# Later, chained residual sums, one unit's sums on VectorE and ScalarE's norms behind its chain, in a convolution and attention kernel on Trainium2

## The chip, the core and the metric

The kernel runs on one core of a Trainium2 chip. The metric is the device time of one execution in microseconds (us), the median of three runs. The core's engines are TensorE (PE in the profile, its weight loads PEld), VectorE (DVE), ScalarE (ACT), GpSimd (POOL) and SyncE (SP), which here only issues DMAs. Each engine runs its instructions in the order of its program: an instruction that waits for a semaphore holds up everything behind it on the same engine.

## What is computed

Eight images of 512 channels by 32x32 pixels go through two layers, all in float32. Cut to what matters:

```
t  = silu(bn(conv1x1(groupnorm(x))));  ys = [t[:256], t[256:]]
for i in 0, 1:                                   # the two blocks
    z = silu(bn(conv3x3(ys[-1])))
    q, k, v = conv1x1(z)                         # 4 heads of 64 channels
    z = softmax(q (k + r) / 8) v                 # over the 1024 pixels
    ys.append(ys[-1] + silu(bn(conv1x1(z))))     # residual sum of conv_m2
x2 = x + silu(bn(conv1x1(concat(ys))))           # residual sum of conv2
out = x2 + permuted_sparse_conv1x1(groupnorm(x2))
```

## The kernel before

**Units.** The attention of one image and block is cut into four units (2 head pairs by 2 halves of the query pixels), 64 units in all. A unit has eight tiles of keys, t = 0 to 7. For each tile TensorE makes the logits of two heads (`lg`, L510), ScalarE copies them to SBUF (`st`, L517), and VectorE takes a running maximum from the PSUM bank (`mx`, L522). After the eighth tile TensorE transposes the maximum, VectorE reduces it (`nm`) and TensorE spreads it (`mb`). Then `soften` on VectorE adds the negated maximum to the tile (L544), `exponent` on ScalarE takes the exponential (L548), GpSimd adds the tile to a running sum in four pieces of 256 columns (`sum`, L555), and TensorE multiplies it with the values (`po`, L562). At the end TensorE reduces the sum over partitions (`den`), ScalarE copies it (`rb`), and VectorE takes the reciprocal and writes the product into `q` (L583 and L585).

**Order of the work.** The unit loop (L1048 to L1086) mixes the softens, exponentials and values of one unit with the logits of the next. Four units form a slot; the images go in pairs, (0,1), (2,3), (4,5), (6,7), each with the slots block 0 of both images and then block 1 of both. Between the tiles of the units a filler (L912) brings in the other work, in steps that a planner's clock paces: `advance` runs generators until a share of the planned time is used, and `clock.at` puts a function off by a planned delay. The filler's work is `conv_m2` of block outputs, the 3x3 convolution as six products (`m` with `plane`, L313), the projection to q, k and v, and a background list: `conv1` of later images, `conv2` and the last convolution of earlier ones.

**Who may pass whom.** A scheduler orders each engine's program by the program's order and its dependencies. Three helpers fix parts of it by hand: `in_turn` chains VectorE's maxima, softens and transform steps, `act_turn` chains ScalarE's copies and exponentials, `pe_turn` chains TensorE's logits, values and transposes. In the kernel before the residual sums and the group norms' `apply` are in none of these chains, so the scheduler puts them where their inputs are due by its plan.

**The lines the change touches.** `apply` (L165) normalises one 128x512 half tile in place on ScalarE, for `norm_x` (L237, the input x) and `norm_x2` (L473, the sum x2). `conv_m2` (L416) loads the residual from DRAM into a tile `res`, multiplies, applies SiLU on ScalarE into `m2s` (L130), and adds on VectorE (L430): into `ybuf` for block 0, in place into `res` for block 1; the sum is stored by SyncE. `conv2` (L443) does the same with `xr` and `cv2s` (L457), then takes group norm statistics (L139), and stores the pair after its second half. `res`, `xr` and the last convolution's `x2r` share a pool `gr` of two buffers; `m2s`, `cv2s`, `y` and `rb` share a pool of three; all 128x512 PSUM results share five banks (`ps_f`). All loads and stores go through SyncE's one queue of instructions. `GroupNorm.mean` and `var` (L141 to L162) end in small VectorE steps on 128x4 numbers (`gms`, `gd`, `gvs`, `go`) and two small matmuls (`gm`, `gv`).

## Time and profile before

| | us |
|---|---|
| three runs | 3157.03, 3156.82, 3152.05 |
| median | 3156.82 |
| the profiled execution | 3162.82 |
| its span, first to last instruction | 3161.1 |

The span holds 34185 instructions. The mean granted TensorE clock is 0.996 of full speed. Apart from PE and PEld, the busy times are: DVE 2049.9 us, ACT 1721.0, POOL 1398.4. In the profile a group line of the timeline reads: start, duration, engine, line of the kernel, operation, output <- inputs by the program's names, shapes, number of instructions; in square brackets the idle time of the engine just ahead of it and what ended that. Times are counted from the span's start. The work of a pair of images repeats with a period of 709 us: a place at 992 us comes again at 1702 and 2411.

### The profile page before, as it was taken

What the parts mean: (1) busy time and instruction counts of PE and PEld (TensorE: products, weight loads), DVE (VectorE), ACT (ScalarE), POOL (GpSimd) and SP (SyncE); (2) the same over time, 40 slices, a digit from 0 to 9 for tenths busy, and PEclk for the clock granted to TensorE, in tenths of its full rate; (3) what the DMA queues carried; (4) which work ended last, traced back from release to release, by engine and by line L of the source; (5) the groups of instructions that cost most, each with busy time, mean ns of one, the idle gap of its engine ahead of it and who ended that gap; (6) DMA issues with size and microseconds to landing.
All of it is one profiled execution on the core that took longest, in us unless ns stands there. A gap on an engine that the chain in (4) does not pass through costs nothing.

```text
span 3161.1 us, 34185 instructions
## 1 busy us (share of the span) xinstructions
PE 3077.0 (97%) x11668; PEld 1515.3 (48%) x11668; DVE 2049.9 (65%) x2718; ACT 1721.0 (54%) x2349; POOL 1398.4 (44%) x1867
## 2 busy tenths in 40 slices
PE   7999999998999999999999999999999999999999
PEld 3645354454445454455445454454445454453333
DVE  5446577567667576667666676767666676767642
ACT  3245765855655555644656455544656455546621
POOL 2104444546444554455444454445444464444520
PEclk9999999999999999999999999999999999999999
DMA  8852352421233232424233332424233332413356
GB/s 289 292 182 74 130 180 87 153 77 63 88 116 131 79 128 71 149 84 148 84 116 130 114 127 70 153 85 136 91 110 130 120 120 70 150 64 120 120 205 217
DMA packets 142014, 399.35 MB, mean 126 GB/s; under 512 B 13072, under 2 KB 14352, under 8 KB 141840
## 3 DMA queue, kind: packets, MB, share of 16 engines
q1 hardware_dynamic: 141120, 396.94, 36.6%
q8 instruction: 92, 1.51, 0.2%
q14 instruction: 82, 0.67, 0.1%
q10 hardware_dynamic: 720, 0.23, 0.0%
HBM read 317.42 MB, written 79.69 MB: 126 GB/s over the span
## 4 chain that ended last, share of the span: by engine, by line
PE 75%; DVE 4%; ACT 4%; issue 2%; DMA 1%; POOL 1%; SPq 0%; ACTq 0%; DVEq 0%; POOLq 0%
PE cv L175 15%; PE m L313 13%; PE po L562 12%; PE lg L510 12%; PE l L175 7%; PE qk L175 6%; PE v L405 3%; PE m L175 3%; PE den L576 2%; PE mb L539 2%; PE mt L530 1%; ACT st L517 1%; DVE st L544 1%; ACT st L548 1%; DVE mx L522 1%
## 5 line engine op out<-in xcount | busy, mean ns | idle before, releaser
L555 POOL TENSOR_TENSOR sum<-sum,st 128x256 f32<-128x256 f32 x1536 | 1132.0, 771 | 552.1 <-ACT st L548 547.7
L522 DVE TENSOR_TENSOR mx<-mx,lg 128x512 f32<-128x512 f32 x768 | 477.8, 682 | 417.6 <-ACT st L517 417.4
L517 ACT COPY st<-lg 128x512 f32<-128x512 f32 x1024 | 525.0, 597 | 356.1 <-PE lg L510 331.7
L548 ACT ACTIVATE st<-st 128x1024 f32<-128x1024 f32 x512 | 539.1, 1068 | 304.1 <-DVE st L544 302.9
L544 DVE TENSOR_TENSOR st<-st,mb 128x1024 f32<-128x1024 f32 x512 | 604.4, 1215 | 60.2 <-PE mb L539 60.2
L555 POOL TENSOR_TENSOR sum<-st,st 128x256 f32<-128x256 f32 x256 | 185.1, 754 | 788.8 <-ACT st L548 788.8
L313 PE MATMUL m<-plane,w_m 128*128 128x256 f32 x2304 | 528.8, 383 | 4.9 <-ACT cv2s L130 2.7
L562 PE MATMUL po<-st,v 128*64 128x512 f32 x2048 | 497.8, 605 | 18.2 <-ACT st L548 16.2
L510 PE MATMUL lg<-q,k 64*128 64x512 f32 x2048 | 510.9, 617 | 2.9 <-ACT y L130 2.9
L313 PEld LDWEIGHTS m<-plane,w_m 128*128 128x128 f32 x2304 | 426.4, 189 | 129.5 <-issue 45.1
L175 PE MATMUL cv<-y,w_cv 128*128 128x512 f32 x1024 | 464.5, 599 | 7.9 <-ACT cv2s L130 4.6
L510 PEld LDWEIGHTS lg<-q,k 64*128 64x128 f32 x2048 | 177.3, 186 | 328.2 <-issue 267.4
L175 PEld LDWEIGHTS cv<-y,w_cv 128*128 128x128 f32 x1024 | 185.8, 190 | 248.1 <-issue 226.4
L562 PEld LDWEIGHTS po<-st,v 128*64 128x64 f32 x2048 | 128.8, 136 | 323.6 <-issue 237.3
L175 PE MATMUL cv<-x,w_cv 128*128 128x512 f32 x512 | 237.0, 610 | 10.6 <-ACT y L130 3.7
L175 PE MATMUL l<-x,w_l 128*128 128x512 f32 x512 | 236.9, 606 | 7.9 <-DVE mx L522 6.9
L175 PE MATMUL qk<-z,w_qkv 128*128 128x512 f32 x512 | 234.0, 600 | 1.4 <-DVE mx L522 1.4
L583 DVE RECIPROCAL rb<-rb 128x256 f32<-128x256 f32 x128 | 215.5, 1723 | 26.0 <-ACT rb L579 25.8
L531 DVE TENSOR_REDUCE nm<-mt 128x4 f32<-128x512 f32 x128 | 82.3, 684 | 144.7 <-PE mt L530 144.7
L579 ACT COPY rb<-den 128x512 f32<-128x512 f32 x64 | 37.3, 583 | 230.4 <-PE den L576 230.4
L175 PEld LDWEIGHTS cv<-x,w_cv 128*128 128x128 f32 x512 | 95.3, 194 | 132.0 <-issue 109.3
L175 PEld LDWEIGHTS l<-x,w_l 128*128 128x128 f32 x512 | 93.4, 191 | 130.4 <-issue 112.2
(145 smaller groups left out, 2408.8 us busy)
## 6 DMA issues: line engine op xcount, KB each, us to landing
w_m<-w_m SPq DMA_DIRECT2D x96, 768.0 KB, 4.8
w_cv<-in_cv SPq DMA_DIRECT2D x90, 512.0 KB, 3.5
y<-y SPq DMA_DIRECT2D x64, 512.0 KB, 4.8
x<-in_x SPq DMA_DIRECT2D x56, 512.0 KB, 5.2
y<-y SPq DMA_DIRECT2D x64, 256.0 KB, 3.5
k<-r SPq DMA_DIRECT2D x32, 512.0 KB, 3.6
res<-y SPq DMA_DIRECT2D x32, 512.0 KB, 4.0
xr<-in_x SPq DMA_DIRECT2D x32, 512.0 KB, 4.1
```

The source lines that it names most:

```text
L175: nc.tensor.matmul(ps, w, moving, start=(n == 0), stop=(n == len(terms) - 1))
L313: nc.tensor.matmul(ps[:, ts(co, 256)].rearrange("p (t x) -> p t x", x=F), w[:, co, c, dx], u[:, 9 * c : 9 * c + 8, dx : dx + F], start=(j ...
L405: nc.tensor.matmul(ps[:, ts(j, P)], z[:, c, ts(4 * j4 + j, P)], w[:, c, 512 + P * hp : 512 + P * hp + P], start=(c == 0), stop=(c == IT - 1),)
L510: nc.tensor.matmul(lg[h], self.k[r, ts(t, P)], self.q[r, self.hp, ts(self.half, HALF)], start=True, stop=True)
L517: act_turn(nc.scalar.copy(st[:, h], lg[h]))
L522: in_turn(nc.vector.tensor_tensor(self.mx[:, h], so_far[:, h], lg[h], ALU.max))
L531: nc.vector.tensor_reduce(self.nm[:, h], mt, AX.X, ALU.max, negate=True)
L544: in_turn(nc.vector.tensor_tensor(st, st, flat(self.mb), ALU.add))
L548: act_turn(nc.scalar.activation(st, st, AF.Exp))
L555: nc.gpsimd.tensor_tensor(flat(self.acc)[:, part], flat(so_far)[:, part], st[:, part], ALU.add)
L562: nc.tensor.matmul(self.po[HD * h : HD * h + HD], self.v[:, t, ts(h, HD)], self.st[t][:, h], start=(t == 0), stop=(t == KT - 1),)
L583: nc.vector.reciprocal(self.rb[:, r], self.rb[:, r])
```

## The change

Residual sums are kept back. A new class `Later` holds a list of closures; each is due a planned delay after it is added (2.0 us of the planner's clock in `conv_m2`, 3.0 in `conv2`), runs in the order of the list, and all that remain are run ahead of the last step of the generator. Each sum is put into VectorE's chain by `in_turn`; its store, and for `conv2` the statistics, come with it. `conv2` now yields after every channel group in the same way. The last of the 64 units adds each tile to its sum with one VectorE instruction of 128x1024 in the chain, where the other units keep four GpSimd instructions of 128x256. The group norms' `apply` gets a dependency of order on the last copy or exponential that ScalarE's chain has emitted so far: it can't run ahead of that instruction. Nothing else is changed; what is computed is the same.

```diff
         def apply(self, k, dst, src):
-            nc.scalar.activation(dst, src, AF.Identity, bias=self.off[:, k : k + 1], scale=self.rstd[:, k : k + 1])
+            return nc.scalar.activation(
+                dst, src, AF.Identity, bias=self.off[:, k : k + 1], scale=self.rstd[:, k : k + 1]
+            )
...
+    def act_behind(instruction):
+
+        if act_last:
+            tc.add_manual_dep(instruction.ins, act_last[0].ins.name, IN_ORDER, reason="order of ScalarE")
+
...
+    class Later:
+
+
+        def __init__(self, delay):
+            self.delay, self.waiting = delay, []
+
+        def add(self, f):
+            self.waiting.append(f)
+            clock.at(self.delay, lambda: self.upto(f))
+
+        def upto(self, f):
+            while f in self.waiting:
+                self.waiting.pop(0)()
+
+        def flush(self):
+            if self.waiting:
+                self.upto(self.waiting[-1])
...
         def norm_x(self, tiles, k=None):
-            for k in range(CT) if k is None else (k,):
-                t = tiles[k // 2][:, k % 2]
-                self.gn0.apply(k, t, t)
+            for j in range(CT) if k is None else (k,):
+                t = tiles[j // 2][:, j % 2]
+                act_behind(self.gn0.apply(j, t, t))
...
             q = self.q
+            later = Later(2.0)
...
                     dst = y_rows(co, h) if i == 0 else res[:, co]
-                    nc.vector.tensor_tensor(dst, res[:, co], t, ALU.add)
-                    load(y_dram[n][2 + i][:, co, ts(h, HALF)], dst)
+
+                    def add(h=h, co=co, dst=dst, src=res[:, co], t=t):
+                        in_turn(nc.vector.tensor_tensor(dst, src, t, ALU.add))
+                        load(y_dram[n][2 + i][:, co, ts(h, HALF)], dst)
+
+                    later.add(add)
+                    if (h, co) == (1, IT - 1):
+                        later.flush()
                     yield us
...
+            later = Later(3.0)
...
                     bn_silu(t, ps, BN_CV2 + co)
-                    nc.vector.tensor_tensor(res[:, c], res[:, c], t, ALU.add)
-                    self.gn1.stats(co, h, res[:, c])
-                    if c == 0:
-                        yield us
-                load(x2_dram[n][:, h, 2 * cp : 2 * cp + 2], res)
-                yield us
+
+                    def add(cp=cp, c=c, co=co, res=res, t=t):
+                        in_turn(nc.vector.tensor_tensor(res[:, c], res[:, c], t, ALU.add))
+                        self.gn1.stats(co, h, res[:, c])
+                        if c == 1:
+                            load(x2_dram[n][:, h, 2 * cp : 2 * cp + 2], res)
+
+                    later.add(add)
+                    if (cp, c) == (1, 1):
+                        later.flush()
+                    yield us
...
             t = tiles[k // 2][:, k % 2]
-            self.gn1.apply(k, t, t)
+            act_behind(self.gn1.apply(k, t, t))
...
                 self.acc = pair(one, "acc", f"sum_{self.name}")
+            if t and self is units[-1]:
+
+                so_far = self.st[0] if t == 1 else self.acc
+                in_turn(nc.vector.tensor_tensor(flat(self.acc), flat(so_far), st, ALU.add))
+                return
             for j in range(4 if t else 0):
```

## The prediction

> **What bounds the kernel now.** I read the busy shares first, then the waits of TensorE in the timeline, stretch by stretch, then what each of them waited for.

> ```profile
> PE 3077.0 (97%) x11668; PEld 1515.3 (48%) x11668; DVE 2049.9 (65%) x2718; ACT 1721.0 (54%) x2349; POOL 1398.4 (44%) x1867
> L544 DVE TENSOR_TENSOR st<-st,mb 128x1024 f32<-128x1024 f32 x512 | 604.4, 1215 | 60.2 <-PE mb L539 60.2
> ```

> TensorE is busy for 3077.0 of 3161.1 us. So all of its idle time is 84 us, and an edit pays or costs only where it moves a TensorE wait. The program's work on TensorE stays the same. The other engines have time to spare on average, but each runs in order: what counts is which instruction stands ahead of the one that TensorE waits for. I therefore compared the built programs' orders on each engine and walked each place where it changed through the timeline. Only the following places move a TensorE wait.

> **Early norms and banks (gain).** In two places a SiLU that frees a PSUM bank stands behind a table load and an exponential (380.33 us: the bank of `y`; 609.73 us: of `m2s`):

> ```profile
> 378.20 1.28 ACT L130 ACT_TABLE_LOAD   x1
> 379.50 0.78 ACT L130 ACTIVATE y<-cv,bn_b,bn_s 128x512 f32<-128x512 f32 x1
> 380.33 1.12 PE L175 MATMUL cv<-x,w_cv 128*128 128x512 f32 x2 [2.16 <-ACT y L130]
> 609.73 2.62 PE L175 MATMUL cv<-x,w_cv 128*128 128x512 f32 x4 [2.13 <-ACT m2s L130]
> ```

> With the norms behind the chain, the built program runs both SiLUs ahead of that exponential, next to another SiLU, and saves two loads of 1.28. The SiLU then ends by 377.5 and 606.1, before TensorE wants the bank, so 2.1 goes at each; what is late next (the exponentials, wanted 3 to 7 us after they end) has slack. Behind 609.73 TensorE also ran at half clock for a 3.4 us stretch (granted 0.64 over 609.7 to 614.5), worth 1.7. Two smaller waits of `y` and `po` (187.41 and 527.14, 1.5 each) lose their cause but meet DMA waits soon after: I take 0.5 of at most 3. Together -6.4 (ends 0 and -9).

> **cv2s ahead of an exponential (gain).** At 1259.53 a bank waits 0.77 for `cv2s`, which now precedes the exponential; three pairs of images: 3 x -0.7 = -2.1 (0 to -2.3).

> **The last unit (gain).**

> ```profile
> 3009.41 16.46 POOL L555 TENSOR_TENSOR sum<-sum,st 128x256 f32<-128x256 f32 x24 [1.20 <-ACT st L548]
> 3016.98 8.90 DVE L150 TENSOR_TENSOR gd_b<-mv_b,gms_b 128x4 f32<-128x4 f32 x1
> 3026.33 0.59 PE L156 MATMUL gv_b<-gd_b,gmat 128*128 128x4 f32 x2 [5.90 <-DVE gd_b L152]
> 3026.78 5.76 PE L175 MATMUL l<-x,w_l 128*128 128x512 f32 x8
> ```

> A subtraction of four columns takes 8.90 us and ends as GpSimd's 24 sums end; TensorE waits 5.90 for it, then does 8 passes in 5.76 where 3.70 is usual. The change takes 28 sums off GpSimd and puts 7 x 1.22 = 8.5 us on VectorE (the duration of a soften, the same shape). Walking VectorE's new order, softens and sums alternate and `gd` is done at 3023.1, so the matmul comes 3.2 earlier; the 8 passes may run at full clock (2.0). The wait that is left, 2.7, is of a size that was followed by half clock at 609.73 and not at 380.33, so I take 1.3 of the 2.0: -4.5 (ends -3.0 and -6.9). What is late next is `den`, for which the last sum ends at 3025.7, before it is wanted.

> [...]

> **Second residual of block 1, images 1, 3, 5 (loss).** This decides. The view is the timeline around 990 us, by engine:

> ```profile
> 984.88 1.23 DVE L430 TENSOR_TENSOR res<-res,m2s 128x512 f32<-128x512 f32 x1
> 991.40 1.22 DVE L544 TENSOR_TENSOR st<-st,mb 128x1024 f32<-128x1024 f32 x1
> 992.53 2.10 DVE L430 TENSOR_TENSOR res<-res,m2s 128x512 f32<-128x512 f32 x2
> 988.49 0.52 SPq L78 DMA_DIRECT2D res<-y  x1
> 987.44 1.06 ACT L548 ACTIVATE st<-st 128x1024 f32<-128x1024 f32 x1
> 988.40 2.03 ACT L517 COPY st<-lg 128x512 f32<-128x512 f32 x4
> 990.30 1.09 ACT L548 ACTIVATE st<-st 128x1024 f32<-128x1024 f32 x1
> 987.14 5.45 PE L313 MATMUL m<-plane,w_m 128*128 128x256 f32 x24
> 992.52 1.94 PE L562 MATMUL po<-st,v 128*64 128x512 f32 x8
> ```

> The second half's `res` takes the first half's buffer, so its load is issued at 988.49, when the first half's store has landed (issued 986.14, 2.33), and lands at 992.40. In the program before, softens 2 and 3 ran from 982.62, ahead of it. In the changed program both stand behind all four sums, and `in_turn` forbids them to pass. The wait that is added is VectorE's, for the load; queued behind it are softens 2 and 3, then maxima and softens 4 and 5. Without the soften ahead, the store is issued some 0.4 earlier: load landed at 992.0, two sums to 993.7, softens to 994.9 and 996.1. Exponential 2 ends at 996.0 instead of 988.50: `po` wants it at 992.52 and waits 3.5. Then ScalarE makes its four copies (2.0), then exponential 3 (1.1): 999.1, where before `po` 3 went at 993.43. TensorE is late by 5.6; the trace has 0.2 of slack at most, I take 5.4. The same rows stand at 1702 and 2411 us: 3 x 5.4 = +16.2. Ends: +3 each if only the first wait stays, +8 if half clock follows it, as behind this wait of 3.0 at 219:

> ```profile
> 219.00:222.40 3.40, 3.39 (x8) 1.18 (x8) 0.00 (x0) 1.25 (x2) 0.00 (x0) 0.50 0.71 248
> ```

> (Columns: window, length, busy time of PE, PEld, DVE, ACT and POOL, clock, DMA.) The cover was 5.45 us of 3x3 products, and it is used up.

> **Block 0, images 3, 5, 7 (loss).**

> ```profile
> 1301.67 1.88 DVE L522 TENSOR_TENSOR mx<-mx,lg 128x512 f32<-128x512 f32 x3 [2.29 <-ACT st L517]
> 1307.08 0.69 DVE L430 TENSOR_TENSOR ybuf<-res,m2s 128x512 f32<-128x512 f32 x1 [3.52 <-DMA res<-y]
> 1316.01 1.98 PE L175 MATMUL l<-x,w_l 128*128 128x512 f32 x4 [2.48 <-DVE mx L522]
> ```

> The third sum waits for its load (1299.82 to 1307.05). Three maxima run ahead of it now; in the changed order all four stand behind it, and the first frees the bank that TensorE takes at 1302.41. The load is issued at 1299.4, one store and not two ahead of it; from the 3.9 us of the load at 988 and the 7.2 of this one I bound its landing by 1303.3 and 1306.6. At 1304 the bank comes at 1305.2: +2.8. The wait at 1316.01 takes about half of that back; then soften 6 stands behind a sum of `xr` that waits for `cv2s`, and the bank wanted at 1323.96 comes some 3 late. So 3 x 3 = +9 (ends 0, if the later waits take it all back, and +5 each).

> **Block 0, images 2, 4, 6 (loss).** The load of `res` lands at 1131.18; softens 4 and 5, which ran at 1121.26 to 1123.61, now stand behind it. The load goes out 1.4 sooner (1124.5); landed at 1129 to 1129.8, exponentials 4 and 5 are in time for `po` at 1135.12, but soften 6, `cv2s` and the plane of `m` follow late: 1141 to 1143 where TensorE began at 1139.89. 3 x 2 = +6 (0 to +3 each).

> **The rest.** Everywhere else the sums of `conv_m2` and `conv2` move by a few places with their inputs long there; the `po` that follows has 3 us of 3x3 products ahead of it, as at 1514.73 to 1520.11. I cost these at nothing; without that cover each would cost one sum, 0.7 to 1.2. The stores and loads move in SyncE's queue with their sums; the store of a `conv2` pair goes out about 1 later, and the pair stored at 1321.41 is not loaded again before 1383.

> **Sum:** -6.4 - 2.1 - 4.5 + 16.2 + 9 + 6 = +18.2 us. The profiled execution took 3162.82, so it would take 3181.0; it lies 6.0 above the median of the runs, 3156.82, from which the sum gives **3175.0**. About 6 us (0.2%) is what a measurement of this kernel can tell from no change.

> **Rivals.**

> (1) *Faster: the cover at 990 us holds.* If the second `res` lands before the softens matter, all four sums pass without a wait, and the same goes for block 0. Place: the load issued at 988.49. Price: the three losses vanish, and -13.0 is left: 3144. It decides at a landing of 988.7: two sums (1.4), soften 2 (1.2) and its exponential (1.1) then end at 992.5, when `po` is wanted. For it: nothing in the change delays that load. Against it: the load would need to land 3.3 sooner than I derive, and it needs the store ahead of it. 0.14.

> (2) *No change.* Only the first wait at 990 stays (+3 x 3) and block 0 costs 1 each (+6): +2.0, 3158.8. It needs the copies of ScalarE to go ahead of exponential 2, against the order of its chain. 0.14.

> (3) *My forecast*, 3164 to 3188. For it: every step is an order that the built program fixes and a transfer whose time is in the trace. 0.52.

> (4) *The clock gate follows.* The waits of 3.5 at 990 and of 2.7 at the end bring half clock (1.7 per stretch of 3.4 us) and the block 0 places cost their upper ends: +8 x 3, +5 x 3, +3 x 3, with the gains of 11.6 (the last unit at -3.0): +36, 3193. 0.15. [...]

> (5) *The last unit gains nothing*, since VectorE's own seven sums hold the subtraction as GpSimd's did: +4.5, 3179.5; inside my range for (3). 0.05.

> **How the numbers follow.** The predicted time is that of (3), 3175. Faster by over 0.2% is (1): 0.14, and I add 0.02 from the edge of (2). Within 0.2% is the rest of (2): 0.12. Slower is (3), (4) and (5): 0.72. The range leaves out (1) and the upper quarter of (4): from 3151, below (2), to 3196.

> **What would show it.** In the profile after: `po` waits of about 3.5 and 2 us for the exponential near 990, 1702 and 2411 (shifted by what came before), VectorE idle there for a DMA of `res` ahead of its sums; the gain at 380 and 610 as missing waits; `gd` no longer 8.90, and `gv`'s wait below 3 us. I am wrong if `po` runs through at 990, if half clock follows these waits (then it is more), or if the early gains come back as DMA waits.

## The result, and the profile after

The changed kernel takes 3203.09 us (median of 4 runs, 3201.45 to 3205.92) where the kernel before took 3155.54 beside it (4 runs): a ratio of 1.0150, 95% interval 1.0137 to 1.0163, so 47.5 us slower. The forecast was 3175, range 3151 to 3196. The profiled execution took 3204.52, 41.7 more than the profiled execution of before; where the other 6 us are is said with the fifth experiment (e5).

The busy times and two costly groups on the page of the changed kernel (L586 is the exponential, L605 the product with the values; the columns at the end are busy time, mean, idle time just before them and what ended it):

```profile
PE 3100.5 (97%) x11668; PEld 1521.7 (48%) x11668; DVE 2041.3 (64%) x2725; ACT 1716.2 (54%) x2345; POOL 1371.9 (43%) x1839
L586 ACT ACTIVATE st<-st 128x1024 f32<-128x1024 f32 x512 | 539.6, 1069 | 353.8 <-DVE st L582 348.9
L605 PE MATMUL po<-st,v 128*64 128x512 f32 x2048 | 509.7, 609 | 33.3 <-ACT st L586 25.4
```

TensorE does the same 11668 matmuls, but its busy time is 23.5 higher, part of which is half clock, as shown below. `po`'s idle time for exponentials went from 16.2 to 25.4, and the exponentials' for softens from 302.9 to 348.9. Of the kernel before (who waited for whom, us in total, times, longest):

```profile
ACT st L548 <- DVE st L544: 302.9, 130, 7.1
PE po L562 <- ACT st L548: 16.2, 14, 3.7
```

To find the rest I compared the start of each TensorE instruction in the two traces and noted each place where the lag, the difference of the two starts, jumps.

**Block 1, images 1, 3, 5: +8.4, +8.2, +8.4, together 25.** The timeline of the changed kernel at the first of them, by engine: VectorE (L458 the residual sum, L582 soften), ScalarE, TensorE.

```profile
982.70 1.28 DVE L458 TENSOR_TENSOR res<-res,m2s 128x512 f32<-128x512 f32 x1 [2.12 <-ACT m2s L130]
990.58 1.29 DVE L458 TENSOR_TENSOR res<-res,m2s 128x512 f32<-128x512 f32 x2 [6.59 <-DMA res<-y]
991.79 2.34 DVE L582 TENSOR_TENSOR st<-st,mb 128x1024 f32<-128x1024 f32 x2
...
993.03 1.06 ACT L586 ACTIVATE st<-st 128x1024 f32<-128x1024 f32 x1 [7.72 <-DVE st L582]
994.00 2.03 ACT L555 COPY st<-lg 128x512 f32<-128x512 f32 x4
995.89 1.09 ACT L586 ACTIVATE st<-st 128x1024 f32<-128x1024 f32 x1
...
994.14 1.97 PE L605 MATMUL po<-st,v 128*64 128x512 f32 x4 [3.67 <-ACT st L586]
997.03 1.97 PE L605 MATMUL po<-st,v 128*64 128x512 f32 x4 [0.92 <-ACT st L586]
```

This is the chain of the prediction, step for step: VectorE stands 6.59 for the load of the second half, the softens come behind it, then an exponential, then ScalarE's four copies, and only then the next exponential; `po` waits twice. The two waits and the overlap between them cost 5.3 to 5.9 at each of the three places (the lag at the second group of `po`). The other 2.5 to 2.9 come behind it, while TensorE runs at half clock. The stretches of the changed kernel around it (length, busy time of PE, PEld, DVE, ACT, POOL, then clock, DMA share, GB/s):

```profile
990.30:994.00 3.70, 0.17 (x1) 0.00 (x0) 3.42 (x4) 0.97 (x2) 0.00 (x0) 0.81 0.58 158
994.00:997.40 3.40, 2.34 (x6) 0.59 (x8) 3.40 (x7) 2.98 (x6) 3.06 (x5) 0.50 0.64 227
997.40:1000.80 3.40, 3.40 (x8) 0.85 (x6) 1.98 (x2) 1.06 (x1) 3.40 (x6) 0.50 0.18 69
```

TensorE is empty for 3.5 us, then works at 0.50 through the next 6.8. The mean of 0.81 over the first 3.70 says that half clock began about 1.4 before its end, at 992.6, when TensorE (last work at 985.02 + 5.45) had been empty for 2.1.

**Block 0, images 3, 5, 7: +4.5, +7.0, +3.4.** VectorE and TensorE of the changed kernel (L560 is the maximum, L177 a convolution, L338 the 3x3 product):

```profile
1313.92 0.69 DVE L458 TENSOR_TENSOR ybuf<-res,m2s 128x512 f32<-128x512 f32 x1 [2.81 <-ACT st L555]
1314.53 2.47 DVE L560 TENSOR_TENSOR mx<-mx,lg 128x512 f32<-128x512 f32 x4
...
1315.27 3.70 PE L177 MATMUL cv<-y,w_cv 128*128 128x512 f32 x8 [2.96 <-DVE mx L560]
1328.33 1.98 PE L177 MATMUL l<-x,w_l 128*128 128x512 f32 x4 [0.95 <-DVE mx L560]
1337.95 3.29 PE L338 MATMUL m<-plane,w_m 128*128 128x256 f32 x14 [1.94 <-DVE x2r L524]
```

All four maxima stand behind the third sum, as predicted. The releaser named at 1313.92 is a ScalarE copy that the sum does not read. The load of `res`, issued at 1308.88, took 5.0 to land, so until 1313.9, and e11 below, without the load, has no wait of `cv` there.

**Block 0, images 2, 4, 6: +3.2, +3.0, +1.4**, a wait of 2.9 of the 3x3 products at 1148.30 and its like. The second sum waits for its load, and from there to the plane that the products read (until 1148.19) VectorE is idle for 0.47 alone:

```profile
1135.86 1.29 DVE L458 TENSOR_TENSOR ybuf<-res,m2s 128x512 f32<-128x512 f32 x2 [4.88 <-DMA res<-y]
1146.95 1.24 DVE L307 TENSOR_TENSOR plane<-a,b 128x544 f32<-128x544 f32 x1
1148.30 2.09 PE L338 MATMUL m<-plane,w_m 128*128 128x256 f32 x7 [2.91 <-ACT st L555]
```

**Places that the prediction does not have: six waits of `qk`, +0.75 each.** VectorE of the changed kernel at the first one (L492 is `conv2`'s sum):

```profile
843.75 1.28 DVE L492 TENSOR_TENSOR xr<-xr,cv2s 128x512 f32<-128x512 f32 x1 [0.66 <-ACT cv2s L130]
844.96 1.21 DVE L582 TENSOR_TENSOR st<-st,mb 128x1024 f32<-128x1024 f32 x1
...
847.82 2.46 DVE L560 TENSOR_TENSOR mx<-mx,lg 128x512 f32<-128x512 f32 x4
```

and TensorE, which wants the bank that the first maximum frees:

```profile
848.54 3.70 PE L177 MATMUL qk<-z,w_qkv 128*128 128x512 f32 x8 [0.48 <-DVE mx L560]
```

In the program before, two softens and only then the sum stand there, and `qk` goes on without a wait:

```profile
842.02 2.35 DVE L544 TENSOR_TENSOR st<-st,mb 128x1024 f32<-128x1024 f32 x2
846.62 1.29 DVE L457 TENSOR_TENSOR xr<-xr,cv2s 128x512 f32<-128x512 f32 x1 [0.66 <-ACT cv2s L130]
848.95 3.27 PE L175 MATMUL qk<-z,w_qkv 128*128 128x512 f32 x7
```

Now the sum, which waits for `cv2s`, goes ahead of both softens, and its statistics go between them.

**Gains.** The stalls at 380.33 and 609.73 are gone (the lag falls by 2.2 and 3.9 there), but around 342 and 400 to 426 the lag rises by 2.4 and 4, at waits that lead back to DMAs of `x`. The bank of `cv2s` gives 0.8 three times.

### The profile page after: what moved, and what is told of

It reads as the page before. It is cut to its first block, busy times and chain, and to the rows that moved or that the text cites. A ratio compares the mean times of both kernels' runs of the same rounds, so it can differ in the third digit from the quotient of the medians.

```text
span 3202.8 us, 34145 instructions
## 1 busy us (share of the span) xinstructions
PE 3100.5 (97%) x11668; PEld 1521.7 (48%) x11668; DVE 2041.3 (64%) x2725; ACT 1716.2 (54%) x2345; POOL 1371.9 (43%) x1839
## 3 DMA queue, kind: packets, MB, share of 16 engines
q8 instruction: 92, 1.51, 0.2%
## 5 line engine op out<-in xcount | busy, mean ns | idle before, releaser
L598 POOL TENSOR_TENSOR sum<-sum,st 128x256 f32<-128x256 f32 x1512 | 1108.1, 767 | 596.3 <-ACT st L586 590.7
L586 ACT ACTIVATE st<-st 128x1024 f32<-128x1024 f32 x512 | 539.6, 1069 | 353.8 <-DVE st L582 348.9
L560 DVE TENSOR_TENSOR mx<-mx,lg 128x512 f32<-128x512 f32 x768 | 476.5, 680 | 386.4 <-ACT st L555 386.1
L555 ACT COPY st<-lg 128x512 f32<-128x512 f32 x1024 | 524.3, 596 | 348.5 <-PE lg L548 322.7
L582 DVE TENSOR_TENSOR st<-st,mb 128x1024 f32<-128x1024 f32 x512 | 603.2, 1211 | 62.2 <-PE mb L577 62.2
L338 PE MATMUL m<-plane,w_m 128*128 128x256 f32 x2304 | 533.9, 386 | 14.6 <-ACT st L555 8.6
L605 PE MATMUL po<-st,v 128*64 128x512 f32 x2048 | 509.7, 609 | 33.3 <-ACT st L586 25.4
L548 PE MATMUL lg<-q,k 64*128 64x512 f32 x2048 | 517.3, 623 | 2.2 <-ACT y L130 2.2
L338 PEld LDWEIGHTS m<-plane,w_m 128*128 128x128 f32 x2304 | 430.2, 191 | 142.5 <-issue 45.1
L177 PE MATMUL cv<-y,w_cv 128*128 128x512 f32 x1024 | 467.9, 602 | 13.8 <-DVE mx L560 8.9
L548 PEld LDWEIGHTS lg<-q,k 64*128 64x128 f32 x2048 | 178.9, 188 | 332.2 <-issue 278.9
L177 PEld LDWEIGHTS cv<-y,w_cv 128*128 128x128 f32 x1024 | 187.0, 191 | 256.2 <-issue 230.8
L605 PEld LDWEIGHTS po<-st,v 128*64 128x64 f32 x2048 | 129.8, 137 | 346.3 <-issue 228.3
L177 PE MATMUL cv<-x,w_cv 128*128 128x512 f32 x512 | 236.5, 609 | 5.1 <-DVE mx L560 2.5
L177 PE MATMUL qk<-z,w_qkv 128*128 128x512 f32 x512 | 235.3, 601 | 2.9 <-DVE mx L560 2.9
L177 PE MATMUL l<-x,w_l 128*128 128x512 f32 x512 | 233.9, 600 | 2.2 <-DVE mx L560 1.0
L626 DVE RECIPROCAL rb<-rb 128x256 f32<-128x256 f32 x128 | 215.3, 1721 | 23.4 <-ACT rb L622 23.3
L177 PEld LDWEIGHTS cv<-x,w_cv 128*128 128x128 f32 x512 | 95.3, 194 | 125.7 <-issue 109.2
L177 PEld LDWEIGHTS qk<-z,w_qkv 128*128 128x128 f32 x512 | 92.5, 190 | 129.4 <-issue 97.2
```

The lines of the kernel that those rows point to most:

```text
L177: nc.tensor.matmul(ps, w, moving, start=(n == 0), stop=(n == len(terms) - 1))
L338: nc.tensor.matmul(ps[:, ts(co, 256)].rearrange("p (t x) -> p t x", x=F), w[:, co, c, dx], u[:, 9 * c : 9 * c + 8, dx : dx + F], start=(j ...
L548: nc.tensor.matmul(lg[h], self.k[r, ts(t, P)], self.q[r, self.hp, ts(self.half, HALF)], start=True, stop=True)
L555: act_turn(nc.scalar.copy(st[:, h], lg[h]))
L560: in_turn(nc.vector.tensor_tensor(self.mx[:, h], so_far[:, h], lg[h], ALU.max))
L582: in_turn(nc.vector.tensor_tensor(st, st, flat(self.mb), ALU.add))
```

## The experiments

The theory after the result: the loss is VectorE's wait for the second half's `res`, put ahead of softens and maxima by the chain. Its rivals: that the sums' new places cost the time, load or no load; that the rest of the change (`conv2`, the norms, the last unit) has a part in it; and that the profile of before was itself off. The kernel before was timed again beside each group of experiments, at 3155.5 to 3159.8, so kernels are compared by their ratios to it; 0.0010 is 3.2 us, and most intervals are 3 to 5 us to each side. A "+56" behind a ratio is the ratio put into microseconds. Lags are taken against the first profile of before, from e5 on against e5's.

**e1_only_conv_m2.** The kernel before with `conv_m2`'s part of the diff alone. Against the changed kernel, three parts are taken back:

```diff
-                act_behind(self.gn0.apply(j, t, t))
+                self.gn0.apply(j, t, t)
...
-            act_behind(self.gn1.apply(k, t, t))
+            self.gn1.apply(k, t, t)
...
-                    def add(cp=cp, c=c, co=co, res=res, t=t):
-                        in_turn(nc.vector.tensor_tensor(res[:, c], res[:, c], t, ALU.add))
...
+                    nc.vector.tensor_tensor(res[:, c], res[:, c], t, ALU.add)
+                    self.gn1.stats(co, h, res[:, c])
+                    if c == 0:
+                        yield us
+                load(x2_dram[n][:, h, 2 * cp : 2 * cp + 2], res)
+                yield us
...
-            if t and self is units[-1]:
+            if False:
```

> Of the change only conv_m2's sums are late and chained; conv2's sums, the norms and the last unit's sums are as before. By the lag of TensorE, instruction by instruction, in the profiles, the places behind conv_m2's residual loads lose 25.0 (block 1), 14.9 and 7.5 (block 0) us. Theory A (the chained sums wait for loads, and half clock follows): all of that comes with this part alone, +40 to +50 us on the kernel before. Theory B (the loss needs the parts together: norms, conv2's sums and these on crowded engines): clearly less, +10 to +30. Theory C (the norms cost it): about 0.

Measured: 3212.01 (3208.16 to 3215.18), ratio 1.0179 (1.0164 to 1.0194), so +56: this part alone costs more than the whole change. Its lag rises at the same places: +8.3, +8.6 and +7.4 in block 1, 2.1 to 3.5 at images 3, 5, 7 of block 0. At images 2, 4, 6 it rises by 4.5 to 7, more than in the changed kernel: there the scheduler puts an exponential and its table load (1.06 and 1.28) ahead of `m2s`, so the first sum ends later, and VectorE's wait for the load ends at 1139.86 against 1135.86, of which 1.6 is lag from earlier places.

**e2_without_conv_m2.** The norms and the last unit alone: `conv_m2` and `conv2` are those of before (`conv2` by the edit of e1).

```diff
-                    def add(h=h, co=co, dst=dst, src=res[:, co], t=t):
-                        in_turn(nc.vector.tensor_tensor(dst, src, t, ALU.add))
...
+                    nc.vector.tensor_tensor(dst, res[:, co], t, ALU.add)
+                    load(y_dram[n][2 + i][:, co, ts(h, HALF)], dst)
```

> The norms behind ScalarE's chain and the last unit's sums on VectorE alone; all residual sums as before. Theory A: the gains that the lag shows are all that is left, -2.1 to -4 early, -2.5 for the banks of cv2s, -6.3 at the end: -9 to -13 us, faster than the kernel before. Theory B: within 5 us of the kernel before. Theory C: slower than before by 20 or more.

Measured: 3152.65 (3147.28 to 3155.47, 10 runs), ratio 0.9982 (0.9968 to 0.9996): -5.7, and by medians 3.9 below the kernel before beside it. I had expected 9 to 13, from three gains; e7 and e8 show that two of them, at the end and at `cv2s`, are not in this part.

**e3_block1_as_before.** The whole change, but block 1's sums are issued at once and outside the chain.

```diff
-                    later.add(add)
-                    if (h, co) == (1, IT - 1):
-                        later.flush()
+                    if i != 0:
+                        nc.vector.tensor_tensor(dst, res[:, co], t, ALU.add)
+                        load(y_dram[n][2 + i][:, co, ts(h, HALF)], dst)
+                    else:
+                        later.add(add)
+                        if (h, co) == (1, IT - 1):
+                            later.flush()
```

> The whole change, but block 1's residual sums are emitted at once and unchained, as before. Theory A: the 25.0 us of the three places near 994, 1721 and 2449 us go, and nothing else: -21 to -28 on the changed kernel, some +17 to +24 on the one before. Theory B: less than -15, since block 0's waits grow when these go.

Measured: 3180.20, ratio 1.0078 (1.0063 to 1.0093), so 22.9 below the changed kernel: block 1's share.

**e4_block1_no_load.** The whole change, but block 1's second half of the residual is not loaded; those sums take `q` as first operand and write into `m2s` (the residual is missing from that half). VectorE's sums, softens and maxima stand there in the order of the changed kernel.

```diff
-                res = pair(gr, "gr", f"res_{name}_{h}")
-                load(res, y_dram[n][1 + i][:, :, ts(h, HALF)])
+                held_back = i == 1 and h == 1
+                if held_back:
+                    res = q[:, :, ts(h, HALF)]
+                else:
+                    res = pair(gr, "gr", f"res_{name}_{h}")
+                    load(res, y_dram[n][1 + i][:, :, ts(h, HALF)])
...
-                    dst = y_rows(co, h) if i == 0 else res[:, co]
+                    dst = y_rows(co, h) if i == 0 else t if held_back else res[:, co]
```

> The whole change with its order, but in block 1 the second half's residual is not loaded: the sum takes q, which is in SBUF, instead, and is stored from the tile of the SiLU (the residual of that half is so left out of the output). The sums stand at the same place of VectorE's program, ahead of softens 2 and 3, and wait for no load. Theory A: po's waits near 994, 1721 and 2449 vanish with their half clock, -20 to -26 on the changed kernel, as in the run that puts these sums back. Theory B (the place in the chain costs it, not the load): -0 to -8.

Measured: 3178.65, ratio 1.0075 (1.0060 to 1.0090), 24.4 below the changed kernel, as much as without the change there. VectorE and TensorE of this kernel (L462 the sum, L586 soften, L609 `po`):

```profile
980.21 1.28 DVE L462 TENSOR_TENSOR m2s<-q,m2s 128x512 f32<-128x512 f32 x2
981.42 2.34 DVE L586 TENSOR_TENSOR st<-st,mb 128x1024 f32<-128x1024 f32 x2
...
981.32 5.45 PE L338 MATMUL m<-plane,w_m 128*128 128x256 f32 x24
986.70 1.94 PE L609 MATMUL po<-st,v 128*64 128x512 f32 x8
```

All four sums are ahead of the softens and `po` goes on without a gap behind the products; the lag is level through all three places. The place alone costs nothing here; the wait for the load, put ahead of the softens, costs it all.

**e5_before_again.** The kernel before, unchanged, profiled a second time.

> The kernel before, unchanged, profiled a second time. In the run with conv_m2's sums alone the last unit's 24 GpSimd sums stood beside the same subtraction, and it took 0.56 us where the first profile of the kernel before has 8.90. Theory D (the 8.90 is a matter of one execution, and of the 6.0 us by which that execution lay above its median): 0.2 to 0.8 here, gv waits under 1 us, and the profiled execution takes some 3151 to 3158 us. Theory E (the kernel before always waits there): 8 to 9 us again, and over 3158.

Measured: one execution of 3153.77. VectorE at the last unit:

```profile
3012.39 0.42 DVE L150 TENSOR_TENSOR gd_b<-mv_b,gms_b 128x4 f32<-128x4 f32 x1
3012.84 0.65 DVE L151 TENSOR_TENSOR gd_b<-gd_b 128x4 f32<-128x4 f32 x1
3013.52 0.65 DVE L152 TENSOR_TENSOR gd_b<-gd_b,mv_b 128x4 f32<-128x4 f32 x1
```

The 8.90 of the first profile is 0.42 here, beside the same GpSimd sums, and `gv` does not wait. Between the two executions of one program the lag is 4.9 by 850 (3.6 of it between 150 and 250) and jumps by 6.0 at `gv`. Half clock is a part of the 4.9: e5 was granted 1.00 over 218.5 to 221.9 and over 605.4 to 610.2, where the first profile has 0.50 (218.5 to 221.9) and 0.64 (609.7 to 614.5). So the profile that I predicted from held waits, and half clock, that do not come in every execution, and its 6.0 above the median was the sign of it. It lies 7.3 above the median of all four runs and the changed kernel's profile 1.4 above its own: that is the 6 between 41.7 and 47.5.

**e6_late_unchained.** The whole change, but `conv_m2`'s sums are kept back without being chained.

```diff
-                        in_turn(nc.vector.tensor_tensor(dst, src, t, ALU.add))
+                        nc.vector.tensor_tensor(dst, src, t, ALU.add)
```

> The whole change, but conv_m2's sums, emitted as late as in the change, are not put into VectorE's chain. In the built program the softens then pass them again. Theory A (the place behind which softens wait for a load): the 47 us of conv_m2's places go, within 4 us of the run without the conv_m2 part, 3149 to 3160. Rival (the later emission, of sums and of their stores and loads, costs by itself): 10 or more above that run.

Measured: 3179.09 (3175.11 to 3180.35), ratio 1.0073 (1.0059 to 1.0087). The expectation of 3149 to 3160 missed. At block 1 it held: the lag is level at all three places. At block 0 the lag still rises, by 2.3 to 4.3 at each of the six, and the six waits of `qk` are there. So the chain is the cause at block 1, and at block 0 it is not alone.

**e7_only_last_unit.** The kernel before with the last unit's sums on VectorE alone: the edits of e1 and e2 without the last one of e1, which leaves of the diff:

```diff
+            if t and self is units[-1]:
+
+                so_far = self.st[0] if t == 1 else self.acc
+                in_turn(nc.vector.tensor_tensor(flat(self.acc), flat(so_far), st, ALU.add))
+                return
```

> Only the last unit's sums on VectorE. Theory D: within 2.5 us of the kernel before in the medians, since the wait that it removes is not in most executions. Theory E: -4.5 to -6.5.

Measured: 3155.21 (11 runs), ratio 0.9997 (0.9988 to 1.0006): nothing clear of noise, as e5 would have it.

**e8_only_conv2.** The kernel before with `conv2`'s part alone, later and chained. Left of the diff:

```diff
-                    nc.vector.tensor_tensor(res[:, c], res[:, c], t, ALU.add)
-                    self.gn1.stats(co, h, res[:, c])
...
+                        in_turn(nc.vector.tensor_tensor(res[:, c], res[:, c], t, ALU.add))
+                        self.gn1.stats(co, h, res[:, c])
...
+                    later.add(add)
```

> Only conv2's residual sums late and chained. In the changed kernel a first projection matmul of k or q starts 0.75 late, six times, since a sum of xr stands ahead of soften 2: +4.5 us. Theory A: +2 to +6, no other place. Rival (conv2's sums have cover, as I costed them): within 2 of the kernel before.

Measured: 3168.93 (3167.16 to 3173.33), ratio 1.0044 (1.0029 to 1.0060): +13.9, above the +2 to +6 that I expected here and the nothing of the prediction. Its lag against e5 rises by 0.65 to 0.75 at six `qk`, 0.8 at three `cv`, 0.6 at `m` of images 2, 4, 6, and by 1.0, 1.7 and 1.7 at `m` of images 3, 5, 7, where the sum of `xr` stands ahead of the plane and soften 6; the bank of `cv2s` gives 0.83 three times. That is some 10 net at these places, and the interval of the +13.9 is 9 to 19. The gain at `cv2s`, which I had put down to the norms, belongs to `conv2`: e2 does not have it.

**e9_only_norms.** The kernel before with the norms' dependency alone.

```diff
-                self.gn0.apply(k, t, t)
+                act_behind(self.gn0.apply(j, t, t))
...
-            self.gn1.apply(k, t, t)
+            act_behind(self.gn1.apply(k, t, t))
```

> The kernel before with the norms' dependency alone. Theory (the parts add up): the norms and the last unit together gave -3.9 and the last unit alone -0.3 of noise, so the norms alone give -2 to -5, about 3152. Rival (the -6.4 of the prediction is right and the company of the last unit hid it): -6 or more, 3150 or below. Second rival (the gains come back whole as waits for DMAs): within 1 of no change.

Measured: 3153.92 (11 runs), 5.9 below the 3159.84 of before beside it, ratio 0.9982 (0.9973 to 0.9991): -5.7. That is e2's ratio, and nearer to the rival's -6 than to the -2 to -5 that I favoured.

**e10_late_conv_m2_conv2_as_before.** e6 with `conv2`'s sums as before (the edit of e1 in `conv2`).

```diff
-                        in_turn(nc.vector.tensor_tensor(dst, src, t, ALU.add))
+                        nc.vector.tensor_tensor(dst, src, t, ALU.add)
...
-                        in_turn(nc.vector.tensor_tensor(res[:, c], res[:, c], t, ALU.add))
+                    nc.vector.tensor_tensor(res[:, c], res[:, c], t, ALU.add)
```

> The changed kernel with the sums of conv_m2 later but not chained, and conv2's sums as before. Its twin with conv2's sums later and chained took 3179.1. Theory (conv2's part costs the same 13.3 in company as alone): 3166, that is +10 over the kernel before, and the projection waits of 0.75 each are gone. Rival (the later sums of conv_m2 cost it all at block 0, conv2's part adds nothing to them): 3175 to 3180. Third (later sums without the chain cost nothing and all was conv2's): 3152 to 3157.

Measured: 3167.14 (11 runs), ratio 1.0022 (1.0013 to 1.0031): +7, and the waits of `qk` are gone; e6 had +23. So `conv2`'s part costs 16 in company, 13.9 alone. What is left rises at images 3, 5, 7 of block 0: 1.5, 4.4 and 3.3. There the third sum, which waits for its load (2.00 at 2015.78), stands ahead of three of the four maxima; in the program before it stands behind three. With the sums kept back the scheduler puts it there, chain or not. Images 2, 4, 6 lose nothing here, so e6's 3 us at each of them come only together with `conv2`'s part.

**e11_block0_no_load.** e4 for block 0: its second half of the residual is not loaded, those sums take `q`. TensorE's and VectorE's orders are those of the changed kernel throughout; ScalarE's is not quite, since at images 2, 4, 6 one exponential goes ahead of `cv2s`.

```diff
-                held_back = i == 1 and h == 1
+                held_back = i == 0 and h == 1
...
-                    dst = y_rows(co, h) if i == 0 else t if held_back else res[:, co]
+                    dst = y_rows(co, h) if i == 0 else res[:, co]
```

(The lines taken out are those of e4.)

> The whole change, but in block 0 the residual of the second half is not loaded: those sums take the second half of q as their first operand, so block 0's output is not the reference's. TensorE's and VectorE's orders are those of the changed kernel, instruction by instruction. Theory (the load, as in block 1): the block 0 places, 14.9 and 7.5 in the changed kernel, cost nothing, 3203 - 22 = 3181 (3177 to 3186). Rival (the place of the sums ahead of maxima and softens costs it, load or no load): 3198 to 3204. Between them, 3187 to 3195: the images 3, 5, 7 lose by the load and the images 2, 4, 6 by the place, or the other way round.

Measured: 3190.39 (3185.07 to 3192.52), ratio 1.0094 (1.0078 to 1.0111): +30 where the changed kernel has +47. It is the middle case. Images 2, 4, 6 lose nothing any more. At images 3, 5, 7, TensorE of this kernel:

```profile
1302.06 3.70 PE L177 MATMUL cv<-y,w_cv 128*128 128x512 f32 x8
1316.30 1.98 PE L177 MATMUL l<-x,w_l 128*128 128x512 f32 x4 [1.53 <-DVE mx L564]
1325.92 4.55 PE L338 MATMUL m<-plane,w_m 128*128 128x256 f32 x13 [1.94 <-DVE x2r L528]
```

The wait of `cv` (2.96 at 1315.27 in the changed kernel) is gone with the load; those of `l` and `m` stay, and 3.7 to 4.2 remain at each place. `conv2`'s sum ahead of the plane is a part (e8 shows 1.0 to 1.7), at image 3 slower products of `m` another (13 in 4.55, where 24 took 5.45 in the kernel before at 987.14, at a clock of 1.00); the rest I put down to the order itself, which no run separates.

**e12_block0_as_before.** The whole change, but block 0's sums are issued as before (the edit of e3 for the other block).

```diff
+                    if i != 1:
+                        nc.vector.tensor_tensor(dst, res[:, co], t, ALU.add)
+                        load(y_dram[n][2 + i][:, co, ts(h, HALF)], dst)
...
```

> The whole change, but block 0's sums of conv_m2 are issued as before, at once and outside the chain. Theory (three independent places): 3203 - 22 = 3181, and within 3 of the kernel that only drops block 0's load. Rival (a kernel late by more at block 0 has the loads of block 1 landed sooner, so the places share one loss): 3190 or more. Second rival (chained sums of block 0 also delay conv2's and the projection): below 3175.

Measured: 3190.96 (3189.88 to 3193.26), ratio 1.0095 (1.0081 to 1.0109), the same as e11. In microseconds it is at the rival's 3190, but the kernel before ran 4.3 above its 3155.5 beside it; by ratios block 0's share is 0.0055, 17 us, not the 22 expected.

**The parts.** By ratios: block 1 22.7 (1.0150 less e3's 1.0078), block 0 17.4 (less e12's 1.0095), `conv2` +13.9 (e8), the norms -5.7 (e9), the last unit -0.9 (e7): +47.4, where the whole change has +47.3. That this closes so well is in part chance: the blocks' shares are what the whole change loses without them, the other three are taken alone. Alone, `conv_m2`'s part costs +56 (e1) and not 40, and the parts taken alone make +64. So each share holds in its company, and the parts depend on each other by some 16 us. Of the kernels run, e2 and e9 beat both, by 0.2% with upper ends of 0.9996 and 0.9991.

## Why the prediction was wrong

The direction was right, and the place that decides was named with its mechanism. The time lies 28 above the forecast and 7 above the range. The step that failed is the third below, the moved sums costed at nothing; the clock at block 1 and the row of the last unit were mis-sized besides. By the steps of the prediction, its sum of +18.2 against the parts' +47.4:

- **Second residual of block 1: +16.2 against 22.7** (25 in the profile). The order, the waits and the engine were as worked out; e3 and e4 confirm them. (The store went out no sooner than before, where 0.4 was taken, and the load landed 0.7 later than derived; the sums behind it took 1.3 and not 1.7, which made up for a part.) What was mis-sized is the clock: the prediction takes 5.4 a place and leaves half clock to a rival, and it followed at all three places, 2.5 to 2.9 each.
- **Block 0: +9 and +6 against 17.4** (14.9 and 7.5 in the profile). The waits were those named, and e11, with the changed kernel's trace, shows that the load is what images 2, 4, 6 wait for. At images 3, 5, 7 the first wait put on 3.4 at full clock and 5.0 and 5.1 where half clock followed it (granted 0.52 and 0.65 over the next 3.4), against 2.8 forecast; the wait of `l` took back 0.5, 1.8 and 2.9; `m` put on 1.7, 3.8 (half clock again, 2064.35 to 2067.77) and 1.2, and part of that is `conv2`'s. So half clock raised two of the three places, and `conv2`'s sum all of them.
- **The rest, costed at nothing: +13.9, or +16 with the 2.1 of `cv2s`.** This is the step that failed. I wrote that the `po` that follows has 3 us of products ahead of it and priced a sum without cover at 0.7 to 1.2. The price was right. The cover was looked for in front of `po`, and the sum holds up something else: the maxima, whose bank TensorE wants next for `qk` and `cv`, and the plane and the step on `x2r` that `m` waits for. There the cover is missing, and in e8 fifteen places paid 0.6 to 1.7 each.
- **The last unit: -4.5 against nothing.** I made the term from one row, 8.90 beside 24 GpSimd sums of 0.73 to 0.75. In e5 the subtraction took 0.42, and 0.56 in e1, 0.29 in e9, beside the same sums: the 8.90 was one execution. A row that stood once, in an execution 6.0 above the median, carried a term.
- **Early norms: -6.4 against -5.7** (interval -8.5 to -2.8). The number is met, its steps only in part. With the norms alone the stall of `y` is gone, but `m2s` stays behind a table load and an exponential, and its bank waits 1.42 where it waited 2.13 (ScalarE and TensorE of e9):

```profile
603.71 1.06 ACT L575 ACTIVATE st<-st 128x1024 f32<-128x1024 f32 x1
606.08 0.78 ACT L130 ACTIVATE m2s<-m,bn_b,bn_s 128x512 f32<-128x512 f32 x1
606.91 5.42 PE L177 MATMUL cv<-x,w_cv 128*128 128x512 f32 x12 [1.42 <-ACT m2s L130]
```

That wait stands in e2, e6, e10 and e12 too, and is gone in the changed kernel and in e1, e3, e4 and e11, where block 0's sums are chained: the gain there is the chain's. And the 1.7 for half clock behind 609.73 was right for some executions only: of the four profiles with the wait of 2.13, those of before and e7 have 0.64 behind it, e5 and e8 1.00. What else is in the 5.7 stays open, since three executions with one and the same order up to 850 (before, e5 and e7) lie up to 6.1 apart there. That the term comes out so near is in part luck.
- **Rivals.** The fourth, half clock behind the waits, is what came to pass at block 1; its 3193 lacked `conv2`'s 14, but held a gain of 3 at the end that wasn't there. That a wait of 3.5 would mostly be followed by full clock was an estimate of mine that no run showed. The waits of 3.29 to 3.84 at block 1 were followed by half clock 3 times in 3 (10.24, 10.24 and 6.83 us of it), at the first of them from 2.1 into the time in which TensorE was empty. I chose 5.4 although the prediction's own rows had half clock behind waits of 3.0 and 2.1.

## What to carry to other kernels

Before a dependency is put on an instruction to keep the order, ask what it waits for: an instruction that may wait for a DMA must not stand ahead of work that feeds the bottleneck, and its store ahead of the next load into the same buffer makes that wait longer (in the changed kernel the store is issued at 984.01 and the load at 986.41). Cover is to be counted for everything behind the moved instruction, the freeing of banks too, and not for its best known reader alone. A wait that stands once in one profile is a term only when a second execution shows it or the period of the work repeats it.

## What the runs showed of the hardware

```profile
1146.17:1149.58 3.41, 1.28 (x6) 1.18 (x7) 3.41 (x6) 3.41 (x6) 2.71 (x4) 1.00 0.52 172
1313.42:1316.83 3.41, 1.56 (x4) 0.85 (x5) 2.91 (x5) 2.61 (x3) 3.29 (x5) 1.00 0.50 123
2037.04:2040.45 3.41, 0.52 (x2) 0.15 (x2) 1.61 (x3) 3.38 (x6) 3.30 (x6) 1.00 0.43 165
2596.82:2600.24 3.42, 1.51 (x8) 0.39 (x4) 3.42 (x5) 3.39 (x5) 2.67 (x4) 1.00 0.35 144
```

TensorE was busy for 1.28 and 0.52 of the 3.41 where half clock followed, and for 1.56 and 1.51 where it did not. At block 1 the pieces ahead of half clock (989.15 to 992.56, and its like) have 1.32, 1.28 and 1.08. In these two profiles the first half-clock stretch, at 88, stands behind a piece in which TensorE was busy throughout (3.41). Of the 1786 full-clock pieces behind it, half clock followed all 18 in which TensorE was busy for up to 1.35, and of the others one alone, with 1.49 (changed kernel, 2060.94); one with 1.49 in the kernel before (1314.09) and all of 1.50 or more were followed by full clock. The six waits of 2.83 to 3.00 differ in this way: the four that half clock followed lie in pieces with 0.52 to 1.28 of work, the two others in pieces with 1.51 and 1.56. What sets the clock these two traces do not show.

A VectorE instruction of four columns took 8.90 us beside 24 GpSimd sums in one execution (the first profile of the kernel before, at 3016.98), and at most 1.30 (eight of each kernel) in the thirteen other profiles. What made it long that once stays open.
